# Attention values divided and turned by VectorE in squares of 32, in place of TensorE's transposes

## The chip, the cores and the metric

The kernel runs on one core of a Trainium2 chip. The metric is the device time of one execution in microseconds (us), the median of several runs. The engines are TensorE (PE in the profile; its weight loads are PEld), VectorE (DVE), ScalarE (ACT), GpSimd (POOL) and the queue of SyncE (SP), which issues most DMAs.

## The reference

The block normalises x (8 batches of 1024 tokens with 256 channels), runs causal attention with 16 heads of 16 channels (rotary positions on queries and keys) and a gated feed-forward network beside it, and adds their product to x:

```python
xn = _layernorm(x, axis=-1)
s = _L0_attn_ref(xn, W_attn, b_attn, W_proj, b_proj)
g = _silu(_L0_ffn_ref(xn, w_gate, w_up, w_down))   # silu(xn wg) * (xn wu), times wd; weights int / 127
x = x + s * g
```

Inside the attention, what matters here is its end:

```python
att = jax.nn.softmax(att, axis=-1)
y = jnp.einsum('bhqk,bhkd->bhqd', att, v)
y = y.transpose(0, 2, 1, 3).reshape(Bx, Tx, C)
return jnp.einsum('btc,cd->btd', y, W_proj) + b_proj
```

All tensors are fp32; the feed-forward weights are integers.

## The kernel before

**Groups, halves and steps.** The heads of a batch are worked on in four groups of four heads (`Group`), so there are 32 groups. The 1024 queries are two halves of 512. The softmax is done in two passes: first the largest score of each query is found (`maxima`, tile `pm`, TensorE at L517, read by VectorE at L526 and L528), then the scores are computed again, transposed, with the maximum already subtracted by extra rows of the operands (`weights`, tile `pw`, L579), and ScalarE takes their exponentials (`e`, L586). The maxima of the next group are computed among the weights of the present one. A group has 12 steps `n`: a half and a block of 128 keys, four for the first half and eight for the second.

**Values.** `values` (L616) multiplies the exponentials with the values of the four heads. Each head has a slot of 32 rows in the tile `av` (128 rows for the four heads, 512 columns for the queries of a half): rows 0 to 15 are the values, row 16 (`HD`) is the sum of the exponentials, because each value tile carries a column of ones. `av` is a single PSUM bank. The values are not computed at each step: `add_values` empties the list `waiting` at steps 0, 4 and 7 (`BEHIND`), so that TensorE multiplies the values of three to five key blocks in one run. The run at step 4 ends the first half of the present group, the run at step 0 the second half of the group before.

**Finishing a half.** At the end of such a run ScalarE copies `av` to SBUF (`avs`, L630). `finish` is put on the list `endings` and is called one step later, after the second bank of that step's first pair of heads: TensorE transposes `avs` in four pieces of 128 by 128 (`py`, L638), which puts queries on partitions, and VectorE takes the reciprocal of the sums (L640) and multiplies (L641) into `y`, the 128-token tiles of the batch.

**Projection.** In the next batch (in the last one, partly at its end), for each pair of token tiles, `transpose_y` loads the residual `res` by SP's queue, transposes `y` back in four pieces (`pyt`, L434) and has ScalarE copy them (`yT`, L436), so that channels lie on partitions; `project_out` (`po`, L445) multiplies with the projection's weights `wp_sb`, and VectorE and GpSimd add the bias, multiply with the gate and add to `res`. For the second half of the last batch this is done by the other `finish(batch)` at the very end (L913 to L943).

**Order.** The order on every engine is written out by hand. `attention` walks through the steps of a group; the pieces of the projections and of the feed-forward (`hidden`, `ph`; `down`, `pd`) and of the next batch's inputs (`pxt`, `pqk`, `pv`) wait in a list `chain`, and `slot` takes as many of them as are due by a plan of TensorE's estimated times: a piece is written as (us, function), and `transpose_y` counts 0.45.

**PSUM.** Two banks for `pw`; three for `max_tile`, which serves the maxima, `py`, `pyt` and a small transpose `pq` of the maxima; one for `av`; two for `fill_tile`, which serves everything in the chain. A tile waits for the last reader of the one that had its bank before.

The weights of the feed-forward are small integers, so the program takes the branch with `exact` set.

Of the kernel before, what the change touches and what calls it, by code (L numbers as in the profile page):

```python
# [9 lines left out]
F32 = mybir.dt.float32  # L10
# [4 lines left out]
ALU = mybir.AluOpType  # L15
AX = mybir.AxisListType

P = 128
HEADS = 16
HD = 16  # L20
SLOT = 32
VS = HD + 1
GROUPS = HEADS // 4
HALF = 512
# [11 lines left out]
def gated_block_kernel(ctx: ExitStack, tc: tile.TileContext, x, wqk, bqk, wv, bv, wp, bp, wg, wu, wd, rope, out):  # L36
    nc = tc.nc
    NB, S, C = x.shape
    NT = S // P
    CC = C // P  # L40
# [3 lines left out]
    QT = HALF // P  # L44
# [30 lines left out]
    def max_tile(name):  # L75
        return ps_pm.tile([P, HALF], F32, tag="pm", name=name)
# [5 lines left out]
    xs = const.tile([P, NT, C], F32, name="xs")  # L82
# [68 lines left out]
    ident = const.tile([P, P], F32, name="ident")  # L151
# [62 lines left out]
    class Batch:  # L214
        def __init__(self, b, exact):
            self.b = b


            self.exact = exact
            self.parts_room = None  # L220
            self.hs = {}
            self.y, self.yT, self.res, self.gates = {}, {}, {}, {}
            self.projected = set()
            self.complete = [0, 0]
# [199 lines left out]

        def transpose_y(self, pair):
            b = self.b
            assert self.complete[pair // 2] == GROUPS
            self.res[pair] = p2.tile([P, 2, C], F32, tag="res", name=f"res_{b}_{pair}")
            nc.sync.dma_start(out=self.res[pair], in_=x[b, ts(pair, 2 * P), :].rearrange("(t p) d -> p t d", p=P))
            py = max_tile("pyt").rearrange("p (c n) -> p c n", c=CC)  # L430
            for c in range(CC):
                for i in range(2):
                    t = 2 * pair + i
                    nc.tensor.transpose(py[:, c, ts(i, P)], self.y[t // QT][:, t % QT, ts(c, P)], ident)  # L434
            self.yT[pair] = p1.tile([P, CC, 2 * P], F32, tag="yT", name=f"yT_{b}_{pair}")
            nc.scalar.copy(self.yT[pair], py)  # L436

        def project_out(self, t):
            b = self.b
            pair = t // 2  # L440
            if t % 2 == 0:
                self.pt = fill_tile("po")
            pt = self.pt.rearrange("p (t d) -> p t d", t=2)
            for c in range(CC):
                nc.tensor.matmul(  # L445
                    pt[:, t % 2, :],
                    self.yT[pair][:, c, ts(t % 2, P)],
                    wp_sb[:, c, :],
                    start=(c == 0),
                    stop=(c == CC - 1),  # L450
                )
# [19 lines left out]
        def project(self, pair):  # L471
            pieces = [(0.45, lambda: self.transpose_y(pair))]
            pieces += [(PIECE, lambda t=t: self.project_out(t)) for t in (2 * pair, 2 * pair + 1)]
            return pieces
# [4 lines left out]
    class Group:  # L479
# [127 lines left out]
        def values(self, half, kb, es):  # L607
# [15 lines left out]
            if kb != last:  # L623
                return None
            avs = p1.tile([P, HALF], F32, tag="avs", name=f"avs_{self.name}_{half}")
            if (self.batch.b, self.g, half) == (NB - 1, GROUPS - 1, 1):
                for engine, part in ((nc.scalar.copy, 0), (nc.vector.tensor_copy, 1)):
                    engine(avs[:, ts(part, HALF // 2)], self.av[:, ts(part, HALF // 2)])
            else:
                nc.scalar.copy(avs, self.av)  # L630
            return lambda: self.finish(half, avs)

        def finish(self, half, avs):
            if self.g == 0:
                self.batch.y[half] = p2.tile([P, QT, C], F32, tag="y", name=f"y_{self.batch.b}_{half}")
            pt = max_tile("py").rearrange("p (t h s) -> p t h s", t=QT, h=4)
            for i in range(QT):
                nc.tensor.transpose(pt[:, i].rearrange("p h s -> p (h s)"), avs[:, ts(i, P)], ident)  # L638
            rec = p2.tile([P, QT, 4], F32, tag="rec", name=f"rec_{self.name}_{half}")
            nc.vector.reciprocal(rec, pt[:, :, :, HD])  # L640
            nc.vector.tensor_tensor(  # L641
                self.batch.y[half][:, :, ts(self.g, 4 * HD)].rearrange("p t (h d) -> p t h d", d=HD),
                pt[:, :, :, :HD],
                rec[:, :, :, None].to_broadcast([P, QT, 4, HD]),
                ALU.mult,
            )
            self.batch.complete[half] += 1

# [252 lines left out]
    def finish(batch):  # L901
# [4 lines left out]
        tiles = range(QT, NT)  # L906
        yT = xs[:, :QT, :].rearrange("p (c a) d -> p c (a d)", c=CC)
        banks = {}

        def transposes(c):  # L910
            pt = max_tile("pyt")
            for t in range(QT):
                nc.tensor.transpose(pt[:, ts(t, P)], batch.y[1][:, t, ts(c, P)], ident)  # L913
            return pt

# [6 lines left out]

        nc.scalar.copy(yT[:, 0], transposes(0))
        while waiting:
# [7 lines left out]
        while delayed:  # L932
            delayed.pop(0)[1]()
        pt = transposes(1)
        for engine, part in ((nc.scalar.copy, 0), (nc.vector.tensor_copy, 1)):
            engine(yT[:, 1, ts(part, HALF // 2)], pt[:, ts(part, HALF // 2)])
        for t in tiles:
            project(t, 1)
            pair, i = t // 2, t % 2
# [150 lines left out]
```

## Time and profile before

| | |
|---|---|
| median of 3 runs | 1547.68 us (1547.12 to 1548.84) |
| profiled execution: its own time | 1544.0 us |
| its span, first to last instruction | 1542.3 us |
| mean granted TensorE clock | 0.984 of full speed |
| HBM read, written | 87.83 MB, 41.94 MB |

The profile is of one execution. Busy time of an engine is the time in which at least one of its instructions runs. Matmuls overlap, and their ends are modelled, so the cost of a short matmul in a stream is better read from the distance between two starts. In a group's row, the last part is the time that the engine stood idle before these instructions and what ended it. In the text below, a "stretch" is the time between two runs of values matmuls.

### The profile page before, as it was taken

How to read it: one execution, taken by the hardware profiler on the slowest of the kernel's cores; microseconds unless marked ns; L12 is line 12 of the kernel's file. 1: busy time of each engine (PE TensorE's matmuls, PEld its weight loads, DVE VectorE, ACT ScalarE, POOL GpSimd, SP SyncE). 2: the span in 40 equal slices, each digit the busy share in tenths (PEclk: the TensorE clock that was granted, in tenths of full speed). 3: DMA queues.
4: the chain of work that ended last, by engine and by line, in shares of the span. 5: the costliest groups of instructions: out<-in, count | busy, mean ns of one | idle time of the engine just before them, and what ended most of it. 6: DMA issues, size and time to landing. Idle time of an engine off the chain costs nothing.

```text
span 1542.3 us, 29412 instructions
## 1 busy us (share of the span) xinstructions
PE 1493.0 (97%) x9793; PEld 1075.3 (70%) x9793; DVE 1091.1 (71%) x3336; ACT 953.7 (62%) x2076; POOL 727.0 (47%) x1435
## 2 busy tenths in 40 slices
PE   4999999999999999999999999999999999999997
PEld 2667767776777766777677876777667776676665
DVE  7875776866777676777677767686776776676753
ACT  3355665676657675566665766567665676665664
POOL 3535443554436443474444734355443643434453
PEclk9788999999999999999999999999999999999999
DMA  8822445434454244543345444443455425345300
GB/s 222 151 43 31 92 109 96 82 53 99 109 106 68 57 104 92 109 77 70 98 77 108 66 97 97 83 91 63 98 110 96 77 43 118 84 77 84 49 30 31
DMA packets 86097, 132.85 MB, mean 86 GB/s; under 512 B 13872, under 2 KB 33840, under 8 KB 85936
## 3 DMA queue, kind: packets, MB, share of 16 engines
q1 hardware_dynamic: 85648, 130.60, 42.3%
q8 instruction: 80, 1.31, 0.4%
q14 instruction: 81, 0.66, 0.2%
q10 hardware_dynamic: 288, 0.27, 0.1%
HBM read 87.83 MB, written 41.94 MB: 84 GB/s over the span
## 4 chain that ended last, share of the span: by engine, by line
PE 88%; DVE 5%; ACT 4%; issue 1%; DMA 1%; POOL 0%; SPq 0%; DVEq 0%; ACTq 0%
PE pw L579 20%; PE pm L517 18%; PE av L616 17%; PE ph L342 11%; PE pqk L243 6%; PE pd L396 6%; PE po L445 3%; PE pv L280 3%; ACT e L586 2%; PE py L638 2%; DVE trash L528 2%; DVE top_far L526 1%; PE pyt L434 1%; PE pxt L231 1%; ACT high L259 1%
## 5 line engine op out<-in xcount | busy, mean ns | idle before, releaser
L586 ACT ACTIVATE e<-pw 128x512 f32<-128x512 f32 (+2 forms) x1280 | 677.4, 558 | 290.3 <-PE pw L579 271.8
L528 DVE CUSTOM_DVE_ANT_0 trash<-pm,mask_q 128x128 bf16<-128x128 f32 (+3 forms) x1024 | 500.6, 489 | 188.2 <-PE pm L517 139.1
L579 PE MATMUL pw<-q_st,k_st 67*128 67x512 f32 (+3 forms) x1536 | 548.0, 389 | 12.6 <-ACT e L586 8.1
L517 PE MATMUL pm<-k_st,q_st 65*128 65x512 f32 (+3 forms) x1536 | 535.1, 387 | 8.3 <-DVE top L528 2.2
L526 DVE TENSOR_REDUCE top_far<-pm 128x1 f32<-128x512 f32 x512 | 338.7, 684 | 188.1 <-PE pm L517 186.8
L593 POOL TENSOR_SCALAR_AFFINE_SELECT e<-e 128x256 f32<-128x256 f32 x512 | 204.9, 407 | 402.1 <-ACT e L586 396.5
L579 PEld LDWEIGHTS pw<-q_st,k_st 67*128 67x128 f32 x1536 | 288.6, 191 | 149.8 <-ACT e L586 69.5
L517 PEld LDWEIGHTS pm<-k_st,q_st 65*128 65x128 f32 x1536 | 282.8, 193 | 75.5 <-DVE top L528 20.9
L373 POOL TENSOR_TENSOR th<-th,ups 128x256 f32<-128x256 f32 x192 | 140.3, 731 | 243.4 <-DVE th L369 237.4
L616 PE MATMUL av<-e,v_most 128*32 128x512 f32 (+3 forms) x2304 | 205.8, 499 | 0.0
L616 PEld LDWEIGHTS av<-e,v_most 128*32 128x32 f32 x2304 | 68.3, 111 | 119.5 <-issue 90.4
L377 POOL TENSOR_TENSOR h_low<-th,h_high 128x256 fp32r<-128x256 f32 x192 | 140.5, 732 | 15.3
L243 PE MATMUL pqk<-xnT,wqk_sb 128*128 128x512 f32 x256 | 134.3, 610 | 0.0
L630 ACT COPY avs<-av 128x512 f32<-128x512 f32 x63 | 36.9, 585 | 155.8 <-PE av L616 155.8
L342 PE MATMUL ph<-xnT_high,wg_sb 128*128 128x256 f32 x384 | 102.1, 288 | 0.0
L342 PE MATMUL ph<-xnT_high,wu_sb 128*128 128x256 f32 x384 | 101.6, 287 | 0.0
L342 PE MATMUL ph<-xnT_low,wg_sb 128*128 128x256 f32 x384 | 100.9, 284 | 0.0
L342 PE MATMUL ph<-xnT_low,wu_sb 128*128 128x256 f32 x384 | 100.7, 284 | 0.0
L396 PE MATMUL pd<-wd_sb,h_high 128*128 128x256 f32 x384 | 98.8, 286 | 1.8 <-POOL h_high L376 1.8
L396 PE MATMUL pd<-wd_sb,h_low 128*128 128x256 f32 x384 | 97.7, 284 | 0.8 <-POOL h_low L377 0.8
L369 DVE SCALAR_TENSOR_TENSOR th<-th,ph 128x256 f32<-128x256 f32 x192 | 79.6, 415 | 24.5 <-ACT ups L358 23.4
L354 ACT ACTIVATE th<-ph 128x256 f32<-128x256 f32 x192 | 73.6, 383 | 37.6 <-PE ph L342 27.8
(113 smaller groups left out, 1814.1 us busy)
## 6 DMA issues: line engine op xcount, KB each, us to landing
q_st<-qk SPq DMA_DIRECT2D x256, 128.0 KB, 4.0
k_st<-qk SPq DMA_DIRECT2D x256, 128.0 KB, 5.1
qk<-high SPq DMA_DIRECT2D x58, 256.0 KB, 2.2
qk<-low SPq DMA_DIRECT2D x58, 256.0 KB, 2.3
xs<-in_x SPq DMA_DIRECT2D x17, 512.0 KB, 7.7
res<-in_x SPq DMA_DIRECT2D x30, 256.0 KB, 4.9
out<-res SPq DMA_DIRECT2D x30, 256.0 KB, 2.3
qk<-parts SPq DMA_DIRECT2D x12, 256.0 KB, 3.4
```

Of the source, the lines that this page charges most:

```text
L243: nc.tensor.matmul(pt, wqk_sb[:, c, ts(i, P)], xnT[:, c, ts(half, HALF)], start=(c == 0), stop=(c == CC - 1),)
L342: nc.tensor.matmul(pt, self.weights[up][:, c, ts(hc, P)], part[:, c, ts(quarter, QU)], start=(c == 0 and i == 0), stop=(c == CC - 1 and i ...
L373: nc.gpsimd.tensor_tensor(h, th, ups, ALU.mult)
L377: nc.gpsimd.tensor_tensor(low, th, high.bitcast(F32), ALU.subtract)
L396: nc.tensor.matmul(pt, h[:, ts(i, P)], self.weights[2][:, hc, :], start=(hc == 0 and n == 0), stop=(hc == HC - 1 and n == len(hs) - 1),)
L517: nc.tensor.matmul(pm[:, ts(i, n)], self.q_st[half][:SHIFT, head, at], self.k_st[keys][:SHIFT, head, :n], start=True, stop=True,)
L526: nc.vector.tensor_reduce(self.top_far[:, head, qt - QT : qt - QT + 1], pm, AX.X, ALU.max)
L528: nc.vector.tensor_tensor_reduce(trash[:, :n], pm[:, ts(i, n)], mask_q[:, HALF - n :], 1.0, MASKED, ALU.add, ALU.max, self.top[:, head, qt ...
L579: nc.tensor.matmul(pw[:, ts(i, n)], self.k_st[kb // QT][:, head, ts(kb % QT, P)], self.q_st[half][:, head, lo:], start=True, stop=True,)
L586: nc.scalar.activation(e[:, first : first + count, :], pw[:, : count * n].rearrange("p (a n) -> p a n", n=n), AF.Exp,)
L593: nc.gpsimd.affine_select(out=e[:, :, :P], in_=e[:, :, :P], pattern=[[0, 2], [1, P]], compare_op=ALU.is_ge, fill=0.0, base=0, channel_mult ...
L616: nc.tensor.matmul(self.av[ts(j, SLOT), lo:], v_sb[:, kb, at * VS : at * VS + SLOT], es[j // 2][:, j % 2, :], start=(kb == 0), stop=(kb == ...
```

## The change

VectorE turns `av` itself, in squares of 32 by 32. Inside a square (one head's slot by 32 queries) rows and columns change places, and the square stays where it is. So after the first turn each partition holds a query of the head whose slot it lies in, and each 32 columns hold one head's 16 values and their sum. VectorE takes the reciprocals of the 16 columns of sums, multiplies, and writes the 16 values of an even group into the first half of each 32 columns of a tile `yq`, those of the odd group that follows into the second half. After the odd group it turns `yq` back, which gives 128 channels (four heads of each of two groups) by 512 queries: one chunk of `yT`, ready for the projection. The tiles `avs`, `y`, `py` and `pyt` are gone, and with them TensorE's transposes (L638, L434, L913) and ScalarE's copies (L630, L436, L923 and L936). The order of the 256 channels is another one, and the rows of `wp` are permuted accordingly on the host. `transpose_y` becomes `load_rest`, which only loads the residual, and counts 0 in the plan. For the last half of the last batch the work is cut into two parts of 256 columns.

```diff
-        def transpose_y(self, pair):
+        def load_rest(self, pair):
             b = self.b
-            assert self.complete[pair // 2] == GROUPS
             self.res[pair] = p2.tile([P, 2, C], F32, tag="res", name=f"res_{b}_{pair}")
             nc.sync.dma_start(out=self.res[pair], in_=x[b, ts(pair, 2 * P), :].rearrange("(t p) d -> p t d", p=P))
-            py = max_tile("pyt").rearrange("p (c n) -> p c n", c=CC)
-            for c in range(CC):
-                for i in range(2):
-                    t = 2 * pair + i
-                    nc.tensor.transpose(py[:, c, ts(i, P)], self.y[t // QT][:, t % QT, ts(c, P)], ident)
-            self.yT[pair] = p1.tile([P, CC, 2 * P], F32, tag="yT", name=f"yT_{b}_{pair}")
-            nc.scalar.copy(self.yT[pair], py)
...
-                    self.yT[pair][:, c, ts(t % 2, P)],
+                    self.yT[t // QT][:, c, ts(t % QT, P)],
...
-            pieces = [(0.45, lambda: self.transpose_y(pair))]
+            pieces = [(0.0 if self.exact else 0.45, lambda: self.load_rest(pair))]
...
-            avs = p1.tile([P, HALF], F32, tag="avs", name=f"avs_{self.name}_{half}")
-            if (self.batch.b, self.g, half) == (NB - 1, GROUPS - 1, 1):
-                for engine, part in ((nc.scalar.copy, 0), (nc.vector.tensor_copy, 1)):
-                    engine(avs[:, ts(part, HALF // 2)], self.av[:, ts(part, HALF // 2)])
-            else:
-                nc.scalar.copy(avs, self.av)
-            return lambda: self.finish(half, avs)
+            return lambda: self.finish(half)
...
-            pt = max_tile("py").rearrange("p (t h s) -> p t h s", t=QT, h=4)
-            for i in range(QT):
-                nc.tensor.transpose(pt[:, i].rearrange("p h s -> p (h s)"), avs[:, ts(i, P)], ident)
-            rec = p2.tile([P, QT, 4], F32, tag="rec", name=f"rec_{self.name}_{half}")
-            nc.vector.reciprocal(rec, pt[:, :, :, HD])
-            nc.vector.tensor_tensor(
-                self.batch.y[half][:, :, ts(self.g, 4 * HD)].rearrange("p t (h d) -> p t h d", d=HD),
-                pt[:, :, :, :HD],
-                rec[:, :, :, None].to_broadcast([P, QT, 4, HD]),
-                ALU.mult,
-            )
+            if odd and batch.yT[half] is None:
+                batch.yT[half] = p1.tile([P, CC, HALF], F32, tag=f"yT_{half}", name=f"yT_{batch.b}_{half}")
+            if not odd:
+                batch.yq[half] = p1.tile([P, HALF], F32, tag=f"yq_{half}", name=f"yq_{self.name}_{half}")
+            yq = batch.yq[half]
+            turned = batch.yT[half][:, chunk, :] if odd else yq
+            count = 2 if (batch.b, self.g, half) == (NB - 1, GROUPS - 1, 1) else 1
+            for part in range(count):
+                of = ts(part, HALF // count)
+                nc.vector.transpose(turned[:, of], self.av[:, of])
+                squares, mine = (t[:, of].rearrange("p (c s) -> p c s", s=SLOT) for t in (turned, yq))
+                n = HALF // count // SLOT
+                rec = p2.tile([P, n], F32, tag=f"rec_{n}", name=f"rec_{self.name}_{half}_{part}")
+                nc.vector.reciprocal(rec, squares[:, :, HD])
+                nc.vector.tensor_tensor(
+                    mine[:, :, ts(odd, HD)], squares[:, :, :HD], rec[:, :, None].to_broadcast([P, n, HD]), ALU.mult
+                )
+                if odd:
+                    nc.vector.transpose(turned[:, of], yq[:, of])
+            batch.complete[half] += 1
...
-        def transposes(c):
-            pt = max_tile("pyt")
-            for t in range(QT):
-                nc.tensor.transpose(pt[:, ts(t, P)], batch.y[1][:, t, ts(c, P)], ident)
-            return pt
...
-        nc.scalar.copy(yT[:, 0], transposes(0))
...
-        pt = transposes(1)
-        for engine, part in ((nc.scalar.copy, 0), (nc.vector.tensor_copy, 1)):
-            engine(yT[:, 1, ts(part, HALF // 2)], pt[:, ts(part, HALF // 2)])
...
-        "wp": np.ascontiguousarray(L0_attn_W_proj),
+        "wp": np.ascontiguousarray(
+            np.asarray(L0_attn_W_proj).reshape(-1, 2, 4, HD, C).transpose(0, 2, 1, 3, 4).reshape(C, C)
+        ),
```

## The prediction

> **What bounds the kernel now.** I read the page's first part, then the groups kept apart by shape, then the waits, then the timeline of one stretch on TensorE and VectorE.
>
> ```profile
> PE 1493.0 (97%) x9793; PEld 1075.3 (70%) x9793; DVE 1091.1 (71%) x3336; ACT 953.7 (62%) x2076; POOL 727.0 (47%) x1435
> ```
>
> TensorE is busy nearly throughout, so instructions taken from it should shorten the run. VectorE's 71% looks like room. The groups (count, then busy us and mean ns of one) give the prices:
>
> ```profile
> L526 DVE TENSOR_REDUCE top_far<-pm 128x1 f32<-128x512 f32 x512 | 338.7, 684 | 188.1 <-PE pm L517 186.8
> L638 PE MATMUL py<-ident,avs 128*128 128x128 f32 x256 | 38.5, 272 | 0.0
> L641 DVE TENSOR_TENSOR y<-py,rec 128x256 f32<-128x256 f32 x64 | 27.2, 425 | 2.7 <-PE pyt L434 0.5
> L434 PE MATMUL pyt<-ident,y 128*128 128x128 f32 x120 | 18.5, 276 | 0.3 <-DVE top_far L526 0.2
> L640 DVE RECIPROCAL rec<-py 128x16 f32<-128x16 f32 x64 | 16.2, 253 | 13.1 <-PE py L638 12.2
> ```
>
> The waits (us in total, times, longest) say who holds TensorE's weight loads up: the exponentials, more than VectorE.
>
> ```profile
> PEld pw L579 <- ACT e L586: 69.5, 213, 0.8
> PEld pm L517 <- DVE top L528: 20.9, 60, 0.9
> PEld pm L517 <- DVE top_far L526: 5.4, 15, 0.8
> ```
>
> But these are sums over unlike stretches. TensorE's values matmuls (av) come in runs of 2.1 to 3.0 us, three to a group of heads. VectorE gets no maxima then, and most of its idle time lies there. After the run that ends a half, its values are finished one step later, in the stretch below (TensorE; start us, us):
>
> ```profile
> 542.39 0.60 PE L638 MATMUL py<-ident,avs 128*128 128x128 f32 x4
> 542.75 0.42 PE L517 MATMUL pm<-k_st,q_st 65*128 65x384 f32 x1
> ...
> 544.05 0.74 PE L517 MATMUL pm<-k_st,q_st 65*128 65x384 f32 x1
> ...
> 544.86 0.34 PE L517 MATMUL pm<-k_st,q_st 65*128 65x384 f32 x1
> ...
> 545.52 0.27 PE L553 MATMUL pq<-ident,parts 128*32 128x128 f32 x1
> 545.70 0.50 PE L517 MATMUL pm<-k_st,q_st 65*128 65x512 f32 x1
> ```
>
> VectorE in the same stretch:
>
> ```profile
> 543.03 0.26 DVE L640 RECIPROCAL rec<-py 128x16 f32<-128x16 f32 x1
> 543.33 0.42 DVE L641 TENSOR_TENSOR y<-py,rec 128x256 f32<-128x256 f32 x1
> 543.67 0.55 DVE L528 CUSTOM_DVE_ANT_0 trash<-pm,mask_q 128x384 bf16<-128x384 f32 x1
> ...
> 545.08 0.56 DVE L528 CUSTOM_DVE_ANT_0 trash<-pm,mask_q 128x384 bf16<-128x384 f32 x1
> ```
>
> The pool pm has three buffers. The maxima at 545.70 take the buffer filled three allocations earlier, at 544.05; VectorE read that at 545.08 and was done at 545.64. TensorE started 0.06 us later: here VectorE releases TensorE. From 543.0 to 551.7 VectorE shows no wait beyond 0.15 us between instructions. What it gains in work here, TensorE waits for.
>
> **What the change removes.** TensorE: 256 transposes of values (64 groups of four), 120 for the projection (30 groups) and 8 at the end. A group costs 0.36 us in the stream (542.39 to the next start at 542.75) and some 0.06 us in the matmul behind it: 0.42. That is 94 x 0.42 = 40 us if TensorE alone decided. ScalarE: 63 copies of 585 ns (avs) and 30 of 590 ns (yT), 55 us. Most lies in ScalarE's waits: at 539.70 the avs copy runs before an exponential that could otherwise start near 539.95 instead of 540.18. I take 0.2 us for each finished half, 13 us in all.
>
> Here a rule speaks against the change. In the stream a transpose takes 89 ns (0.36 over four). The Trainium skill, "VectorE: DVE Perf Modes", section "Rules for kernel authors", prefers TensorE for a 128x128 transpose whose result may lie in PSUM; its section "The three transpose paths" gives 390 ns by TensorE and 311 by VectorE, alone and in bf16. By the page's price 384 transposes are 150 us; by the row they are 34. I take the row.
>
> **What it adds.** VectorE, for each half of a group of four heads: one 128x512 turn out of PSUM, a reciprocal of 16 columns, a 128x256 multiplication, and in the 32 odd groups' halves a second 128x512 turn. The trace has no such turn. Nearest row: TENSOR_REDUCE over 128x512 from PSUM, 684 ns. From below: 0.42, by the 128x256 rows, were two elements moved per step; from above: 1.3, at half rate. The page's 311 ns for 128 columns fits the rows' slope: 0.31 plus 384 columns at the slope between the 290 and 689 ns of the maxima's 128 and 512 columns, 0.71. I take 0.69 for both kinds. Reciprocal and multiplication keep 0.25 and 0.42: same sizes, SBUF instead of PSUM as source. An even half then takes VectorE 0.72 us longer (0.69 and a gap of 0.03), an odd one 1.44.
>
> **What it moves, at no cost.** The values' single bank av is read by VectorE one step later instead of by ScalarE at once. The next av run starts 5 us or more after today's reciprocal, which covers it; without that, VectorE's lag of about 2 us would stand before the run. Each yT half has one buffer, written in the next batch's second group, some 20 us after the last projection read it. The residual's load is issued at the same place of SP's queue. POOL gets nothing. The piece now counts 0 in the planner instead of 0.45: neighbours slide, 2 us either way.
>
> **The sum.** I carry two delays through each stretch: VectorE's (added work, less 0.2 for ScalarE's copy, less any wait before today's reciprocal, less its later waits) and TensorE's (0.63 early: 0.42 and 0.2, unless a pm buffer comes later). In the stretch shown the half is odd: VectorE is late by 1.44 - 0.2 = 1.24. The maxima at 545.70 had 0.06 to spare and go 1.2 late; nothing later wins that back. One batch (467 to 650 us) has eight finished halves:
> - second halves, ending in the long stretches after the 2.97 us runs: +0.1 (even; a wait of 0.43 before the reciprocal is used up), +1.2 (odd), +0.5 (even, no such wait), +0.8 (odd, with a projection's transposes gone). Together +2.6.
> - first halves, in the stretches of 10 us: +0.5 (even, where normalisation for the next batch keeps VectorE full), -0.3 (odd, wait 0.32), -0.5 (even), +0.1 (odd). Together -0.2.
> - two projection groups in stretches without a finish, where VectorE has some 4 us idle: -0.4 each, -0.8.
>
> Per batch +1.6; six batches +9.6. The first batch, without most projections: +2. The last: two halves with VectorE idle, -1.2; the projections' groups there, -1.2; the end -2.0: between the last av (about 1529.85) and the second projection matmuls (1533.27) now lie copies, four transposes, reciprocal, multiplication, four transposes and copies, 3.4 us; after, VectorE's last part is done about 2.8 us behind the av, and with the first chunk's transposes (0.44) gone the stores come some 2 us sooner. Sum: 9.6 + 2 - 4.4 = +7. The profiled execution took 1544.0 us (span 1542.3), so 1551; the median of the runs shown stands 3.7 above it, so 1554.7, say 1555.
>
> **The rivals.**
> 1. TensorE and ScalarE keep their gain (faster). For it: the waits put 69.5 us on ScalarE and only 26.3 on VectorE, and both removed kinds serve the first. Mechanism: VectorE absorbs the turns in its av idle time, because the three buffers, no longer shared with py and pyt, let TensorE run ahead. Whole, this is 40 + 13 us: 1495; with half to three quarters of it lost in the odd halves, 1520 to 1535. It decides where a turn costs below about 0.59 us: in my sum 0.1 us less per turn is worth about 1 us a batch, 8 us in all. Against it: the 0.06 us above, found once in each long stretch. Chance 0.27.
> 2. The turn runs at half rate, 1.25 us (slower). 96 turns x 0.56 = 54 us more on VectorE, some 70% of it felt: 1555 + 38 = 1593. Nothing in the trace excludes it; the page's price speaks against. Chance 0.08.
> 3. The lag also holds the two fill buffers (feed-forward, projections), which VectorE releases: 0.3 us for each of 64 halves, +19: 1574. Chance 0.12.
> 4. Nothing felt: what is freed and what is added cancel within the stretches: 1548. Chance 0.13.
>
> **How the numbers follow.** My own case has 0.40, 1547 to 1565. A measurement of this kernel can tell about 0.2% (3.1 us) from no change. Faster takes rival 1 and little else: 0.27. Same takes rival 4 and the low end of my case: 0.15. Slower: 0.58. The range reaches into rival 1's partial case and over rival 3: 1528 to 1580; rival 2 and the whole of rival 1 lie outside.
>
> **What would show it.** Right: turns of 0.65 to 0.75 us; VectorE near 1155 us; TensorE's instruction count down by 384 and its idle time in the long stretches up; waits of pm for VectorE's rows well above 26 us, waits of pw for the exponentials below 69.5; odd halves' stretches longer by about 1 us, those without a finish shorter. Wrong: TensorE's waits for VectorE unchanged, each batch shorter by 4 us or more, or a turn below 0.5 us.

## The result, and the profile after

The changed kernel takes 1626.45 us (median of four runs, 1618.01 to 1633.05) against 1547.4 us of the kernel before (four runs, 1541.16 to 1548.84): ratio 1.0516, 95% interval 1.0459 to 1.0573. It is slower by 80 us; the prediction said slower by 7, with 1580 as the end of its range. The profiled execution took 1626.06 us, with a span of 1624.3 us, 82.0 us over that of before.

The page of the changed kernel: first each engine's busy time, share and instructions, then the granted TensorE clock in tenths, in 40 slices of the span.

```profile
PE 1523.5 (94%) x9409; PEld 1068.3 (66%) x9409; DVE 1163.5 (72%) x3434; ACT 907.7 (56%) x1980; POOL 732.3 (45%) x1435
PEclk9799899999999999998999989999899998989799
```

TensorE has 384 instructions fewer and is busy 30 us longer. That is the first sign that its instructions themselves became slower. The second row shows where: there are eights all along the span, where the kernel before had them only at its start. The mean clock fell from 0.984 to 0.951.

The groups by shape (count, then busy us and mean ns of one) give the prices that were estimated:

```profile
L637 DVE STREAM_TRANSPOSE yq<-av 128x512 f32<-128x512 f32 x32 | 22.6, 705 | 0.0
L646 DVE STREAM_TRANSPOSE yT<-yq 128x512 f32<-128x512 f32 x31 | 22.0, 711 | 1.1
L642 DVE TENSOR_TENSOR yq<-yT,rec 128x256 f32<-128x256 f32 x31 | 16.4, 529 | 1.1
L642 DVE TENSOR_TENSOR yq<-yq,rec 128x256 f32<-128x256 f32 x32 | 16.1, 502 | 1.1
L642 DVE TENSOR_TENSOR yq<-yT,rec 128x128 f32<-128x128 f32 x2 | 1.5, 734 | 0.1
```

A turn takes 0.71 us, from PSUM and from SBUF alike. The multiplication has grown from 425 ns to 502 and 529, and the two short ones at the end of the kernel, of half the size, take 734.

The waits (us in total, times, longest) that answer to those shown of before:

```profile
PEld pw L572 <- ACT e L579: 77.7, 226, 0.8
PEld pm L510 <- DVE top L521: 50.1, 72, 2.6
PE pm L510 <- DVE top L521: 31.5, 32, 2.4
PEld pm L510 <- DVE top_far L519: 21.6, 55, 1.6
```

TensorE's weight loads now wait 71.7 us for VectorE's maxima instead of 26.3, and the longest single wait is 2.6 us instead of 0.9. The waits for the exponentials did not fall, although ScalarE lost its copies. Another 22.4 us, 1.9 before, are put down to ScalarE's `rows`; one wait so named, shown below, ends in truth with VectorE's work, so 71.7 us may be too little:

```profile
PEld pm L510 <- ACT rows L548: 22.4, 29, 1.3
```

Now the stretch of the prediction, in the same place of the same batch. VectorE (start us, us):

```profile
561.26 0.71 DVE L637 STREAM_TRANSPOSE yT<-av 128x512 f32<-128x512 f32 x1
562.01 0.25 DVE L641 RECIPROCAL rec<-yT 128x16 f32<-128x16 f32 x1
562.30 0.60 DVE L642 TENSOR_TENSOR yq<-yT,rec 128x256 f32<-128x256 f32 x1
562.94 0.71 DVE L646 STREAM_TRANSPOSE yT<-yq 128x512 f32<-128x512 f32 x1
563.57 0.52 DVE L521 CUSTOM_DVE_ANT_0 trash<-pm,mask_q 128x384 bf16<-128x384 f32 x1
...
565.40 0.55 DVE L521 CUSTOM_DVE_ANT_0 trash<-pm,mask_q 128x384 bf16<-128x384 f32 x1
```

TensorE in that stretch; the brackets hold the idle time before the matmul and what ended it:

```profile
564.16 0.44 PE L510 MATMUL pm<-k_st,q_st 65*128 65x384 f32 x1 [0.87 <-DVE top L521]
...
564.96 0.27 PE L546 MATMUL pq<-ident,parts 128*32 128x128 f32 x1
565.95 0.78 PE L510 MATMUL pm<-k_st,q_st 65*128 65x512 f32 x1 [0.72 <-ACT rows L548]
566.52 0.63 PE L572 MATMUL pw<-q_st,k_st 67*128 67x256 f32 x2
566.95 0.42 PE L342 MATMUL ph<-xnT_high,wg_sb 128*128 128x256 f32 x1
567.16 0.41 PE L342 MATMUL ph<-xnT_low,wg_sb 128*128 128x256 f32 x1
```

VectorE's finish occupies it from 561.26 until the next maximum starts at 563.57. The maxima behind it come late, and TensorE stands idle twice, 0.87 and 0.72 us. The second wait is put down to ScalarE, but VectorE's maxima of 565.40 end at 565.95, when the matmul starts. So far this is the prediction. What it did not have comes after 566: the feed-forward matmuls stand 0.21 us apart, from start to start. In the stretch of before it was 0.12:

```profile
546.27 0.28 PE L342 MATMUL ph<-xnT_high,wu_sb 128*128 128x256 f32 x1
546.39 0.28 PE L342 MATMUL ph<-xnT_low,wu_sb 128*128 128x256 f32 x1
```

A table of stretches (span of the stretch, then busy time of PE, PEld, DVE, ACT and POOL, granted clock, DMA share, GB/s) shows it. First the long stretch of before, from the start of one values run to the start of the next, then the same stretch of two batches of the changed kernel:

```profile
536.33:551.82 15.49, 15.49 (x106) 10.39 (x105) 11.28 (x42) 9.00 (x22) 7.90 (x18) 1.00 0.74 162
```

```profile
365.02:382.26 17.24, 15.77 (x102) 10.12 (x101) 13.21 (x44) 8.81 (x22) 8.30 (x18) 1.00 0.59 109
555.02:576.86 21.84, 20.26 (x102) 13.40 (x101) 13.68 (x44) 9.40 (x22) 9.39 (x21) 0.77 0.43 94
```

The batch at 365 runs at full clock and takes 1.75 us more than before, where the prediction gave it 1.2. The batch at 555 has the same instructions and takes 6.35 us more: for 10.2 us its clock was halved, which by the difference of the two (21.84 and 17.24) costs 4.6 us.

Why one and not the other? In the records of every kernel here the clock changes only on a fixed grid of 3.413 us. The Trainium skill, "TensorE: Matmul & The Clock Gate", section "What's actually happening", has windows of this length: activity is judged over free-running windows of 3413 ns. Here are the grid's windows around the two waits, of the batch at 365 (whose idle times, 0.87 us up to 374.16 and then 0.26 and 0.35 us up to 375.95, lie in different windows) and of the batch at 555 (where both lie in one):

```profile
371.44:374.85 3.41, 2.54 (x16) 2.07 (x14) 2.80 (x7) 1.90 (x4) 1.92 (x5) 1.00 0.91 141
374.85:378.27 3.42, 2.81 (x19) 2.10 (x18) 3.13 (x11) 1.93 (x6) 0.41 (x1) 1.00 0.26 91
...
562.60:566.00 3.40, 1.82 (x13) 1.34 (x12) 3.17 (x9) 1.83 (x6) 0.84 (x3) 1.00 0.24 81
566.00:576.20 10.20, 10.20 (x28) 7.37 (x29) 5.54 (x15) 3.19 (x7) 5.18 (x11) 0.50 0.08 28
```

TensorE busy 2.54 and 2.81 of 3.41 us: the clock stays. Busy 1.82 of 3.40: the next three windows have half the clock, although TensorE is busy throughout them. The page's section "HAM oscillation — how this bites in real kernels" gives as abstract rule that gaps of more than some 3.4 us must be avoided; by it neither gap would have cost any clock. In this trace two gaps of 0.87 and 0.72 us in one window were enough; the measurement decides.

The batch at 555 is no single case. From there on the starts of this stretch (555.02, 749.66, 944.22, 1138.87 and 1333.35) lie 194.5 to 194.7 us apart in five batches, and 57 windows of 3.413 us are 194.6. So each batch meets the grid at nearly the same place, and all five lose 10.2 us to half clock in this stretch. Whether the falls themselves hold the batches in step, or this is chance, was not tested.

Over the whole span the records show half clock for 163 us instead of 51. At half the clock TensorE-bound work takes twice as long, so 112 us more of it are up to 56 of the 82 us (by the 4.6 us that 10.2 us cost above, an estimate of 50). By parts (an estimate; the time at half clock counted half):

| part | longer by, us | more at half clock, us | longer at full clock, us | predicted |
|---|---|---|---|---|
| start, before the first values | 0.0 | -1.1 | 0.6 | 0 |
| first batch | 9.8 | 11.3 | 4.2 | 2 |
| six batches between | 62.6 | 77.8 | 23.7 | 9.6 |
| last batch and end | 9.7 | 23.7 | -2.2 | -4.4 |
| sum | 82.1 | 111.7 | 26.3 | 7.2 |

### The profile page after: what moved, and what is told of

The parts are those of the page before. It is cut to its first block, busy times and chain, and to the rows that moved or that the text cites. A ratio compares the mean times of both kernels' runs of the same rounds, so it can differ in the third digit from the quotient of the medians.

```text
span 1624.3 us, 28613 instructions
## 1 busy us (share of the span) xinstructions
PE 1523.5 (94%) x9409; PEld 1068.3 (66%) x9409; DVE 1163.5 (72%) x3434; ACT 907.7 (56%) x1980; POOL 732.3 (45%) x1435
## 4 chain that ended last, share of the span: by engine, by line
PE 72%; DVE 13%; ACT 5%; POOL 5%; issue 2%; DMA 1%; SPq 0%; ACTq 0%; POOLq 0%; DVEq 0%
PE av L609 16%; PE pm L510 15%; PE pw L572 15%; PE ph L342 8%; PE pqk L243 6%; PE pd L396 5%; DVE trash L521 4%; ACT e L579 3%; PE pv L280 3%; PE po L438 3%; DVE top_far L519 1%; DVE yq L642 1%; DVE yT L646 1%; POOL e L586 1%; POOL h_low L377 1%
## 5 line engine op out<-in xcount | busy, mean ns | idle before, releaser
L579 ACT ACTIVATE e<-pw 128x512 f32<-128x512 f32 (+2 forms) x1280 | 679.9, 558 | 511.1 <-PE pw L572 493.3
L510 PE MATMUL pm<-k_st,q_st 65*128 65x512 f32 (+3 forms) x1536 | 553.4, 399 | 54.5 <-DVE top L521 31.5
L572 PE MATMUL pw<-q_st,k_st 67*128 67x512 f32 (+3 forms) x1536 | 554.1, 395 | 14.0 <-ACT e L579 11.0
L572 PEld LDWEIGHTS pw<-q_st,k_st 67*128 67x128 f32 x1536 | 298.0, 198 | 162.7 <-ACT e L579 77.7
L510 PEld LDWEIGHTS pm<-k_st,q_st 65*128 65x128 f32 x1536 | 288.1, 198 | 136.9 <-DVE top L521 50.1
L609 PE MATMUL av<-e,v_most 128*32 128x512 f32 (+3 forms) x2304 | 213.5, 507 | 0.9
L243 PE MATMUL pqk<-xnT,wqk_sb 128*128 128x512 f32 x256 | 144.1, 651 | 0.0
L396 PE MATMUL pd<-wd_sb,h_high 128*128 128x256 f32 x384 | 106.7, 304 | 1.9 <-POOL h_high L376 1.9
L396 PE MATMUL pd<-wd_sb,h_low 128*128 128x256 f32 x384 | 105.3, 299 | 0.9 <-POOL h_low L377 0.9
L521 DVE DVE_READ_ACCUMULATOR2_ANT top<- 128x1 f32 x1024 | 84.5, 83 | 0.0
```

The costliest lines, as they stand in the source:

```text
L243: nc.tensor.matmul(pt, wqk_sb[:, c, ts(i, P)], xnT[:, c, ts(half, HALF)], start=(c == 0), stop=(c == CC - 1),)
L396: nc.tensor.matmul(pt, h[:, ts(i, P)], self.weights[2][:, hc, :], start=(hc == 0 and n == 0), stop=(hc == HC - 1 and n == len(hs) - 1),)
L510: nc.tensor.matmul(pm[:, ts(i, n)], self.q_st[half][:SHIFT, head, at], self.k_st[keys][:SHIFT, head, :n], start=True, stop=True,)
L521: nc.vector.tensor_tensor_reduce(trash[:, :n], pm[:, ts(i, n)], mask_q[:, HALF - n :], 1.0, MASKED, ALU.add, ALU.max, self.top[:, head, qt ...
L572: nc.tensor.matmul(pw[:, ts(i, n)], self.k_st[kb // QT][:, head, ts(kb % QT, P)], self.q_st[half][:, head, lo:], start=True, stop=True,)
L579: nc.scalar.activation(e[:, first : first + count, :], pw[:, : count * n].rearrange("p (a n) -> p a n", n=n), AF.Exp,)
```

## The experiments

The theory at the start: VectorE's finish, one step behind the values run, holds the maxima back; TensorE's waits for them cost little themselves but halve its clock. The rivals: the clock is a consequence that costs little, and the time is VectorE's added work; or something else is late (the multiplication, the planner's order, TensorE's freed time). All twelve runs, with the time at half clock from the records of each one's single profiled execution:

| kernel | us | ratio to before, 95% | half clock, us |
|---|---|---|---|
| changed kernel | 1626.45 | 1.0516 (1.0459 to 1.0573) | 163 |
| 1 TensorE's gaps filled | 1596.02 | 1.0357 (1.0308 to 1.0406) | 70 |
| 2 before, with turns added | 1596.79 | 1.0366 (1.0334 to 1.0398) | 69 |
| 3 second turn later | 1581.23 | 1.0274 (1.0223 to 1.0324) | 106 |
| 4 as 3, finish at once | 1536.27 | 0.9965 (0.9945 to 0.9986) | 37 |
| 5 planner's 0.45 back | 1629.94 | 1.0551 (1.0508 to 1.0594) | 200 |
| 6 as 4, with 0.45 back | 1526.64 | 0.9893 (0.9856 to 0.9929) | 96 |
| 7 as 6, multiplication on GpSimd | 1508.38 | 0.9787 (0.9756 to 0.9817) | 63 |
| 8 as 6, reciprocals in PSUM | 1515.91 | 0.9830 (0.9800 to 0.9861) | 69 |
| 9 reciprocals in PSUM alone | 1614.47 | 1.0462 (1.0427 to 1.0497) | 144 |
| 10 finish at once alone | 1545.96 | 1.0041 (1.0026 to 1.0055) | 67 |
| 11 spare transposes on TensorE | 1617.34 | 1.0518 (1.0462 to 1.0575) | 142 |
| 12 before, with its finish at once | 1580.87 | 1.0245 (1.0223 to 1.0267) | 63 |

**1. TensorE's gaps filled.** In the step where the two waits lie, TensorE repeats matmuls that it has to do anyway (weights of step 2 four times, the transpose of the maxima seven times).

```diff
-                for i in range(count):
+                for i in [i for i in range(count) for _ in range(times)]:
...
-                        group.shift_queries(1)
+                        group.shift_queries(1, 7 if busy else 1)
```

> The changed kernel with more TensorE work: in step 2 after an odd group's second half, each matmul of pw for the first pair is issued four times instead of once and the small transpose pq seven times (same results, about 1.3 us of work in each of 15 places, where TensorE stood idle for about 1.6 us). Theory (the waits for VectorE leave TensorE half idle in a 3.4 us window, and the clock is then halved for 3.4 or 10.2 us): the time at half clock falls from 162 us to 80 or less, and the kernel gets faster although work is added: 1575 to 1600 us. Rival 1 (VectorE's added 68 us are paid as such, the clock only follows): 1625 to 1645, low clock or not. Rival 2 (TensorE's transposes kept its activity up, and without them the clock falls): faster too; this run does not tell it from the theory.

1596.02 us, ratio 1.0357 instead of 1.0516: work added to TensorE makes the kernel some 25 us faster, and the time at half clock falls from 163 to 70 us. In the six batches between the first and the last, the stretch of the prediction is longer than before by 1.3 to 2.3 us; in the changed kernel it was 5.8 to 6.4 in five of them and 1.8 in one. This is what the theory asks. It also shows that the clock is not all: with half clock nearly as in before, 3.6% remain.

**2. The turns alone, in the kernel before.** VectorE turns `avs` in place, once in even and twice in odd groups, without use; everything of before stays.

```diff
             avs = p1.tile([P, HALF], F32, tag="avs", name=f"avs_{self.name}_{half}")
...
+            for _ in range(1 + self.g % 2):
+                nc.vector.transpose(avs, avs)
```

> The kernel before, with all of TensorE's transposes and ScalarE's copies, and with VectorE turning the SBUF copy avs in place after each finished half, once for even groups and twice for odd ones (the results of these turns are not used): only the added work. Theory: VectorE's burst makes TensorE wait in the long stretches of odd groups, the clock halves there as in the changed kernel: 1600 to 1660 us, time at half clock 130 us or more. Rival 2 (the clock falls because TensorE's transposes are gone): clock at 0.98, 1555 to 1580. Rival 1: 1590 to 1615 with the clock at 0.98.

The group of the added turns:

```profile
L649 DVE STREAM_TRANSPOSE avs<-avs 128x512 f32<-128x512 f32 x96 | 67.6, 704 | 1.1
```

67.6 us of VectorE's work cost 55 us of time, with only 18 us more at half clock. The theory is missed in both its figures, the half clock (130 us or more) and, narrowly, the time (1600 us or more); rival 1 is met in both. So VectorE's added work has a price of its own. An estimate of what the removed work pays for it: the span of this kernel is 51.2 us over that of before, 42 with the additional half clock counted half; the changed kernel is 26 over it when counted so. The removed transposes and copies pay back some 16 of the 42 us, where alone they were 40 us of TensorE's stream.

**3. The second turn later.** In odd groups the turn back is put at the start of the next values run.

```diff
-                if odd:
+                if odd and count == 2:
                     nc.vector.transpose(turned[:, of], yq[:, of])
...
+            if odd and count == 1:
+                backs.append(back)
...
+                    turn_back()
                     add_values(len(waiting))
```

> The changed kernel with the odd groups' second turn (yq back to yT) moved on VectorE to the start of the next run of values matmuls, where VectorE is idle for 1 to 2 us; same number of instructions. Theory: an odd half's burst is then like an even one's: odd long stretches about 0.8 us longer than before the change instead of 6.3 and 2.8; time at half clock 50 to 80 us; 1550 to 1580. Rival 1 (VectorE's total work decides): 1610 to 1630, since the work is the same.

1581.23 us, ratio 1.0274 instead of 1.0516: some 37 us gained by moving 31 turns of 0.71 us, 22 us of work. The stretch of the prediction is 0.8 us longer than before where the clock stays. Both figures of the theory are missed, the time by 1 us and the half clock, at 106 us instead of 50 to 80, by more.

**4. The finish at once.** As 3, and the finish is called right behind the values run instead of one step later.

```diff
                     add_values(len(waiting))
+                    while endings:
+                        endings.pop(0)()
```

> As the run before, and each half is also finished by VectorE right behind its run of values matmuls instead of one step later, where VectorE waits for TensorE's next maxima anyway. Theory: the even halves' waits go too, what TensorE saved (94 groups of transposes at 0.42 us) comes through in part: 1515 to 1550, time at half clock about 50 us. Rival 1: 1600 or more. If the first maxima behind the run are held up instead: 1560 to 1580.

1536.27 us: the loss is gone, with the same instructions. Half clock is down to 37 us, but this is of the fastest of the twelve executions (1523.42 us, mean clock 0.988). The others have a mean clock of 0.975 to 0.984, which makes some 49 to 77 us at half clock (an estimate: twice the missing share of the span), as much as in before or more. In this run the multiplication stood out. VectorE, then GpSimd, over the same time:

```profile
487.95 1.34 DVE L642 TENSOR_TENSOR yq<-yq,rec 128x256 f32<-128x256 f32 x1
```

```profile
486.37 1.28 POOL L452 TENSOR_TENSOR o<-o,gate 128x512 f32<-128x512 f32 x1
487.72 1.29 POOL L453 TENSOR_TENSOR res<-res,o 128x512 f32<-128x512 f32 x1
```

A multiplication of 0.42 us takes 1.34 us here while GpSimd multiplies and adds. In this kernel, of the 65 multiplications the 22 beside a tensor operation of GpSimd take 866 ns in the mean, the other 43 take 422.

**5. The planner's 0.45 back.** The piece that loads the residual counts 0.45 again, so that its neighbours stand where they did in before.

```diff
-            pieces = [(0.0 if self.exact else 0.45, lambda: self.load_rest(pair))]
+            pieces = [(0.45, lambda: self.load_rest(pair))]
```

> The changed kernel with one number put back: the piece that loads the residual counts 0.45 in the planner of TensorE's time as before, instead of 0, so that the pieces of the chain stand where they stood. Theory: in the changed kernel two stretches of each batch (the long one after group 0, and the one after the first half of group 0 at step 7) are 1.4 and 0.7 us longer in all runs so far, whatever was done to the turns, because six matmuls of the down projection and some of the hidden layer slid; with the number back both go to about 0 and -0.4: about 17 us less, 1600 to 1615. Rival (the slide costs nothing, the burst does): 1620 to 1632.

1629.94 us, not to be told from the changed kernel: the theory's 1600 to 1615 us is missed and the rival's time met. But the two stretches moved much as the theory said: in the first group's long stretch +0.6 us instead of +1.4, in its stretch without a finish -0.4 instead of +0.7 where the clock stays. What was won there, 1.9 us a batch (0.3 of it lost again in other stretches), was lost to half clock elsewhere (200 us instead of 163). A small shift on TensorE's side moves the gaps against the grid, and here that cost as much as the shift won.

**6. Both: finish at once, second turn later, 0.45 back.**

> The kernel of e4_soon (finished behind the run, second turn at the next run) with the planner's 0.45 back. Theory: 12 to 17 us less than e4_soon: 1515 to 1527. Rival (the slide costs nothing): as e4_soon, 1530 to 1540.

1526.64 us, 10 us below 4: with the early finish the planner's old cost is worth something. Half clock is 96 us; some 24 of the 45 us above before lie in the last batch.

**7. The multiplication on GpSimd.** As 6.

```diff
-                nc.vector.tensor_tensor(
+                nc.gpsimd.tensor_tensor(
                     mine[:, :, ts(odd, HD)], squares[:, :, :HD], rec[:, :, None].to_broadcast([P, n, HD]), ALU.mult
                 )
```

> As e6_soon_slide, with the multiplication by the reciprocals on GpSimd instead of VectorE (65 instructions of about 0.73 us there, 0.42 to 1.34 us less on VectorE each). If VectorE's time behind the run is what is still late: 5 to 15 us less than e6_soon_slide, 1505 to 1520. If GpSimd's queue then holds up the masks of the exponentials and the feed-forward: 1525 to 1545.

1508.38 us (1507.26 to 1511.89), the fastest of all, ratio 0.9787 (0.9756 to 0.9817): faster than before, though the interval leaves open whether by 2%. The multiplication costs 0.62 us there:

```profile
L642 POOL TENSOR_TENSOR yq<-yq,rec 128x256 f32<-128x256 f32 x32 | 19.9, 621 | 54.6 <-DVE rec L641 54.6
```

**8 and 9. The reciprocals in PSUM.** They are written into columns of `av` that the turn has read, so that the multiplication has one input in SBUF and one in PSUM; 8 as 6, 9 with nothing else changed.

```diff
-                rec = p2.tile([P, n], F32, tag=f"rec_{n}", name=f"rec_{self.name}_{half}_{part}")
+                rec = self.av[:, part * (HALF // count) : part * (HALF // count) + n]
```

> As e6_soon_slide, with the reciprocals written into the av bank in PSUM, free by then, so that the multiplication has one input in SBUF and one in PSUM. Theory (with both inputs in SBUF it waits for GpSimd's instructions: 421 ns where none runs, 0.6 us and up to 1.34 us where one does): all multiplications take 0.42 us, VectorE has 7 to 10 us less, 1510 to 1522. Rival (the long ones have another cause, the strided columns or the pool of buffers): they stay, and the time is that of e6_soon_slide.

> The changed kernel with nothing but the reciprocals written into the av bank in PSUM, so that the multiplication reads one input from SBUF and one from PSUM. Theory (each burst is 0.2 to 0.75 us longer than predicted wherever GpSimd works, and the longer waits help to halve the clock): all 65 multiplications at 0.42 us, 7 us less on VectorE, 1600 to 1620. Rival (the burst is long enough without it): 1620 to 1630.

The groups of 9:

```profile
L642 DVE TENSOR_TENSOR yq<-yT,av 128x256 f32<-128x256 f32 x31 | 13.0, 421 | 1.1
L642 DVE TENSOR_TENSOR yq<-yT,av 128x128 f32<-128x128 f32 x2 | 0.6, 288 | 0.1
```

Every multiplication is back at 0.42 us, and the two short ones at 0.29, whatever GpSimd does. So it is the second input from SBUF that contends with GpSimd. The Trainium skill, "SBUF — State Buffer", section "Who interferes with whom", states this rule (two inputs in SBUF against a GpSimd instruction that reads SBUF); the sizes are of these runs. Whole kernel: 1614.47 us in 9 (its interval still touches that of the changed kernel), 1515.91 us in 8 (0.983 against 0.9893; these intervals touch too, but all four executions of 8, up to 1518.14, lie below all four of 6, from 1523.55). Two batches of 9 repeat the finding on the clock, with idle times of 0.69 and 0.72 us in both:

```profile
569.50:572.91 3.41, 2.83 (x14) 1.86 (x12) 3.27 (x10) 2.68 (x6) 2.56 (x6) 1.00 1.08 123
572.91:576.32 3.41, 2.58 (x17) 2.27 (x18) 2.98 (x12) 1.38 (x4) 0.31 (x2) 1.00 0.50 146
951.79:955.20 3.41, 2.00 (x14) 1.53 (x13) 3.12 (x9) 2.06 (x6) 0.94 (x3) 0.99 0.57 111
955.20:965.44 10.24, 10.24 (x29) 7.40 (x30) 5.67 (x15) 3.32 (x8) 5.17 (x11) 0.50 0.08 27
```

In the first batch a border of the grid (572.91) falls at the end of the first gap (up to 573.01), so that the second lies in the next window; in the second batch both lie in one. The stretch from values run to values run takes 16.90 us in the one and 21.68 in the other: 10.2 us at half clock cost 4.8 us.

**10. The finish at once, alone.** The two lines of 4 and nothing else: the second turn stays behind the multiplication.

> The changed kernel with each half finished right behind its run of values matmuls, the odd groups' second turn still directly behind the multiplication. Theory (VectorE is idle there, and the three pm buffers cover some 1.5 us of the odd burst of 2.1 us): even stretches as in e4_soon, odd ones 0.5 to 1.5 us longer than there; time at half clock 40 to 90 us; 1540 to 1570. Rival (only the later second turn took the clock's loss away): 1590 or more.

1545.96 us, ratio 1.0041: one step earlier on VectorE's queue takes back some 73 us, nearly the whole loss; a gain over before it is not yet. VectorE in the stretch of the prediction, and the group of its first turn with the idle time before it:

```profile
534.62 0.72 DVE L637 STREAM_TRANSPOSE yT<-av 128x512 f32<-128x512 f32 x1 [1.97 <-PE av L609]
535.38 0.26 DVE L641 RECIPROCAL rec<-yT 128x16 f32<-128x16 f32 x1
535.66 0.42 DVE L642 TENSOR_TENSOR yq<-yT,rec 128x256 f32<-128x256 f32 x1
536.12 0.71 DVE L646 STREAM_TRANSPOSE yT<-yq 128x512 f32<-128x512 f32 x1
536.76 0.39 DVE L521 CUSTOM_DVE_ANT_0 trash<-pm,mask_q 128x256 bf16<-128x256 f32 x1
```

```profile
L637 DVE STREAM_TRANSPOSE yT<-av 128x512 f32<-128x512 f32 x31 | 22.2, 718 | 52.3 <-PE av L609 52.3
```

The turn now starts when the values are done, out of VectorE's idle time, and ends 2.2 us later, before the maxima of the steps that follow. In the changed kernel the idle time before the same group is 0.0: four maxima stand between the run and the finish, and the finish between them and the ones that TensorE needs next.

**11. Spare transposes.** The changed kernel with four transposes of the identity into an unread buffer of the pm pool for each half.

```diff
+            pt = max_tile("py")
+            for i in range(QT):
+                nc.tensor.transpose(pt[:, ts(i, P)], ident, ident)
```

> The changed kernel with four transposes of the identity back on TensorE at each finished half, into a pm buffer that nobody reads: TensorE's removed work without VectorE's or ScalarE's part. Theory (e2_turns lost the clock less often because these transposes kept TensorE above half busy in the 3.4 us window that holds the wait): time at half clock at most 100 us, 1595 to 1615, although 27 us of TensorE work are added. Rival (TensorE's own work has nothing to do with it): 160 us or more at half clock, 1630 to 1650.

Inconclusive: neither the theory (at most 100 us at half clock, 1595 to 1615 us) nor the rival (160 or more, 1630 to 1650) is met. 1617.34 us; by the ratio (1.0518) it is where the changed kernel is. The half clock went from the first odd group's long stretch (now +1.0 to +1.8 us in the six batches between) and grew in the other's (3.4 to 10.2 us a batch); in all it is 142 us. Filling a gap moves the clock's loss, but four short transposes do not remove it.

**12. The kernel before, with its own finish at once.** For groups 1 to 3.

```diff
                     add_values(len(waiting))
+                    while endings and group.g != (0 if n else 1):
+                        endings.pop(0)()
```

> The kernel before, with its own finish of a half (TensorE's four transposes, reciprocal, multiplication) put right behind the values run, as the two kernels with an early finish have it; only the halves of groups 1 to 3 (48 of 64), since those of group 0 need a tile that is still read. It asks whether the early place alone gains, with nothing of the change in it. Theory: it does not. The transposes stand on TensorE and need ScalarE's copy of 0.59 us, which can start only when the last values matmul is done; so TensorE waits 0.6 to 0.9 us behind 48 runs, some 30 to 40 us, and wins back about 1 us in the odd long stretches at most: 1560 to 1590, ratio 1.01 to 1.03. In VectorE's own turn nothing on TensorE waits for the copy, and the early place is free only there. Rival: the place is worth the same to both kernels (VectorE is idle behind the run whoever turns the values), TensorE has other matmuls of the run's step to cover the copy: 1515 to 1540, ratio 0.98 to 0.995, the long second halves shorter by 0.5 to 1 us.

1580.87 us, within what the theory gave; the rival is out. The wait that it named:

```profile
PEld py L638 <- ACT avs L630: 47.5, 47, 1.1
PE py L638 <- ACT avs L630: 34.9, 47, 0.8
```

The six batches between are 3.6 to 4.5 us longer each, without any more half clock. In before the finish stands a step later for a reason: its transposes are on TensorE and need ScalarE's copy. In the changed kernel nothing of the finish is on TensorE, and the place behind the run becomes free. With both kernels at the late place the change costs 5.2% (1.0516); with both at the early place it gains 2.0% (1.0041 over 1.0245, though 12 moves 48 of the 64 halves and 10 all).

## Why the prediction was right or wrong

**Right: which engine decides.** "What it gains in work here, TensorE waits for" holds. VectorE releases TensorE behind the finish in the long stretches, the waits for VectorE's rows rose from 26.3 to 71.7 us, TensorE's freed time did not pay, and the run is slower. That is not luck: at full clock too the parts sum to 26 us more.

**Right: the prices of the turn.** 0.69 us was taken, 0.71 came. This excludes rival 2, and takes away rival 1's condition, a turn below 0.59. For TensorE's transposes the sum took the 89 ns of the trace; by the 390 ns of the Trainium skill, "VectorE: DVE Perf Modes", section "The three transpose paths", they would have been worth 150 us (an estimate), and the sum would have pointed to a faster kernel.

**Right: most stretches at full clock.** Predicted and measured, typical batch: the odd group's long stretch of the prediction +1.2 and +1.8 (the one batch of the six at full clock); the other odd group's +0.8 and +1.0 (one batch of experiment 9, at full clock); third group's +0.5 and +0.8; first halves +0.5, -0.3, -0.5, +0.1 and +0.4, -0.1, -0.5, +0.3; two of the stretches without a finish -0.5.

**Wrong: a term is missing.** The step that failed is the carrying of two delays through each stretch: TensorE's waits were counted at their own length, and its clock was taken as unchanged without a word. Two waits in one window of 3.41 us were followed by half the clock for what comes after. 112 us more at half clock, worth up to 56 of the 82 us, were in no rival, and the range ended at 1580. Without this term the sum would have been off but inside the range: 1544.0 plus the 26.3 us at full clock, plus the 3.7 to the median, is 1574. "Nothing later wins that back" was taken as the worst case, and the delay grew. Shown: the two pairs of like stretches (17.24 and 21.84; 16.90 and 21.68 us) and experiment 1. Not shown: the exact condition for a fall. TensorE's busy share in a window, as the profile models it, does not settle it: in experiment 8 the window at 283.1 us, busy 2.60 of 3.40 us, was followed by half clock, which the one above with 2.54 of 3.41 was not. Over the 14 traces, of the full-clock windows on the grid that were busy less than half, 67 of 69 were followed by half clock; of those busy 0.5 to 0.8, 96 of 344.

**Mis-sized: the planner's slide.** "Neighbours slide, 2 us either way" was the estimate for the whole kernel. The first group's long stretch came out at +1.4 instead of +0.1, its stretch without a finish at +0.7. That is about 2 us a batch, some 14 of the 19 us by which the full-clock sum is above the prediction. Experiment 5 takes 1.9 us of it back in these two stretches where the clock stays, so the slide is shown as their cause; in the whole time its gain was lost to the clock.

**Mis-sized: the multiplication.** "Same sizes, SBUF instead of PSUM as source" was taken to cost nothing. All multiplications together took 33.9 us instead of 27.2, and up to 1.2 us for a single one. In the long stretch this is 0.1 to 0.3 us (17.24 against 17.1 us in the same batch of experiment 9 and 16.90 in the next, all at full clock), and at the end of the kernel two of 0.73 instead of 0.29 us lie on the path. The end was predicted 2.0 us sooner and came 0.7 sooner; in experiment 9 it came 1.4 sooner. Half clock differs there too (4.6 us of it before, 3.5 after, 2.4 in experiment 9), so what the multiplication alone costs at the end stays open.

**Wrong in "what would show it": the waits of pw.** They rose from 69.5 to 77.7 us. The 55 us of copies left ScalarE, but its exponentials wait for TensorE's `pw`, and TensorE was late: ScalarE's idle time that ended so rose from 271.8 to 493.3 us.

**Small: rival 3.** The fill buffers' waits for VectorE are in sum about 5 us, not 19. Rival 4 is out by the result.

**Not weighed at all.** The prediction took the place of the finish on VectorE's queue as given, although it says itself that most of VectorE's idle time lies beside the values runs, one step earlier. The change can gain (how much of it comes from TensorE's freed time and how much from ScalarE's was not separated): with the finish at once, the second turn deferred, the old cost in the planner and the multiplication on GpSimd it is 33 us faster than before.

## What to carry to other kernels

When work moves from an engine that waits for inputs to one that holds buffers, its place in the new engine's queue must be chosen again: put it where that engine stood idle, not where the old one needed it. Count gaps on TensorE by windows, not by length alone: here two short waits close together (1.6 us) cost three times what they lasted (4.6 us). And when a source moves from PSUM to SBUF, look at what GpSimd does at the same time before keeping the old price.

## What the runs showed of the hardware

- The granted clock changes on a grid of 3.413 us that runs free of the program. Windows with TensorE busy 1.82 of 3.40 us were followed by half clock for one or three windows (for three although TensorE was then busy throughout), one with 2.54 of 3.41 was not; but one with 2.60 of 3.40 was (experiment 8), so the busy share alone does not decide. The same stretch of the same kernel costs 17.2 or 21.8 us, and in experiment 9, with the same two idle times, 16.9 or 21.7, by where the grid's border falls.
- A VectorE multiplication of 128x256 with both inputs in SBUF takes 0.42 us alone and up to 1.34 us beside GpSimd's tensor operations; with one input in PSUM always 0.42 us.
- A turn of 128x512 in fp32 on VectorE takes 0.71 us from PSUM and from SBUF, so about the time of a maximum over the same tile.
